# Attention with expert layers on one core: the sums of heads, their reciprocal and the division moved to other steps, and kept copies given fixed places

## The chip, the core and the metric

The kernel runs on one core of a Trainium2 chip. The core's engines run side by side, each in the order of its own queue: TensorE (matmuls; the profile's PE, its weight loads PEld), VectorE (DVE), ScalarE (ACT), GpSimd (POOL) and SyncE (SP), which issues DMAs. The metric is the device time of one execution in microseconds. Before the change the median of 14 runs is 1340.41 us (1339.85 to 1341.01).

## The reference

For `x` of 4 x 512 tokens by 512 features, in float32, the kernel computes `x + attention(xn) + experts(xn)`, where `xn` is the layer norm of `x`.

```
scores  = clip(einsum("bhqd,bhkd->bhqk", q, k), -80, 80), causal mask
weights = softmax(scores / sqrt(192))
out     = (weights @ v) of 16 heads, joined, @ W_O.T
output  = shared_expert(xn) + sum over the 3 best of 7 experts, weighted
expert  = (silu(x @ w1) * (x @ wg)) @ w2
```

Each head's `q` and `k` have 128 features from latent projections and 64 features with a rotary turn (the rope).

## The kernel before

The kernel has an expert part (to about 657 us) and an attention part (from there to the end). It is written in a language that allocates tiles and sets the semaphores. `keep(...)` pins an instruction behind everything that was written before it for its engine, so the order on TensorE, VectorE and ScalarE is that of the code. The GpSimd fetches `yg` (L1664) are kept too, yet the planner has placed them between other GpSimd instructions; where they stand is read from the trace.

**Products.** A 512-wide matrix product is done as seven half-size products (`seven`) in the order p = 0, 1, 5, 4, 6, 2, 3, each of 8 matmul passes, into three PSUM banks. Some of them have their bank copied to SBUF by ScalarE before the bank is added to (`kept`, L297 in the expert part; L1605 in the attention part). In the expert part every kept copy takes a buffer of the tag `v`, five in rotation. `unit_out` (L1045) adds the copies `v[3]` and `v[5]` in place and sends the sum to DRAM. If few units are needed, `y_few` is copied out by ScalarE (one half) and VectorE (the other half, L1386).

**Attention.** There are 32 steps, one for each pair of heads of each batch. Step i does, on TensorE: `scores(i)` (L1432 with 128 rows, then L1443 with 64 rows, into the banks `a0`, `a1`, `b0`, `b1`, `c` and one of a pool), the queries of step i+1 (`pqr` L1282, `pq` L1297), and `values` of step i-1 (`av` L1513). VectorE clips the six score tiles (L1461), ScalarE takes the exponentials (L1465), GpSimd masks (L1469) and adds up each head's weights along the keys (`su`, L1493 and L1497). VectorE also multiplies for the rope of step i+1 (L1268 and four of L1271), and GpSimd subtracts (L1272).

Four heads (two steps) make a project q = 0 to 15. `sums(q)` (L1532) has four matmuls with a column of 32 ones each, one for each head's `su`, into bank `a0`; VectorE takes the reciprocal (L1534); `spread_by_dma` (L1544) sends each head's 32 rows to 128 with four DMAs on SyncE's queue, 16 in all. `divide(q)` multiplies the four heads of `og` by it (L1566, four) and makes the factors of the seven products (L1572 and three of L1575). `project_out(q)` does the seven products (`op`, L230) into the banks `b1`, `c`, `b0`; ScalarE keeps four copies; VectorE adds three banks to `acc` (L1615), GpSimd adds the kept copies (L1612). `combine` (L1677, three on VectorE) adds expert rows that `fetch` (L1664, three indirect DMAs of GpSimd) brought. At the end of `project_out` SyncE loads the next project's factors `m` (L1585).

Order in the main loop, for an even step i = 2q+2: `scores`, `pqr`, `pq`, `weights`, then `sums(q)`, reciprocal and broadcasts, then the rope, `values`, `project_out(q-1)`. For the odd step 2q+3: `scores`, `pqr`, `pq`, `weights` with the rope behind the clips, `values`, and last `divide(q)`. Project 14 is divided in step 31; project 15 is summed inside `project_out(14)` (`last_heads`) and spread by matmuls.

Of the kernel before, what the change touches and what calls it, by code (L numbers as in the profile page):

```python
# [10 lines left out]
F32 = mybir.dt.float32  # L11
# [7 lines left out]
P = 128  # L19
B, S, D = 4, 512, 512  # L20
# [22 lines left out]
def kernel(  # L43
# [87 lines left out]
    def rows(src):  # L131
        return src.rearrange("(c p) f -> p c f", p=P)

    def ffn_in(at, name, w, x_of, between, step=FC):

        hp = fps.tile([P, S], F32, tag="h", name=f"h_{name}")
        gp = fps.tile([P, S], F32, tag="g", name=f"g_{name}")
        for ps, wt in ((hp, w[0]), (gp, w[1])):
            for f in range(FC):
                for c in range(DC):  # L140
                    keep(
                        nc.tensor.matmul(  # L142
                            ps[:, ts(f, P)],
                            wt[:, c, ts(f, P)],
                            x_of(c),
                            start=(c == 0),
                            stop=(c == DC - 1),
                        )
                    )
            if ps is hp:  # L150
                between()
        sl = sw.tile([P, S], F32, tag="v", name=f"sl_{name}", bufs=5)
        keep(nc.scalar.activation(sl, hp, AF.Silu))
        cols = [t.rearrange("p (c n) -> p c n", c=FC) for t in (gp, sl)]

        for f in range(0, FC, step):
            keep(nc.vector.tensor_mul(*(t[:, f : f + step] for t in (at, *cols))))
        return at
# [85 lines left out]
    def load_in(dst, src):  # L244

        with tc.issue_after(last[0]) if last[0] is not None else nullcontext():
            last[0] = nc.sync.dma_start(dst, src).ins
# [40 lines left out]
    def product(name, tag, a, w, done, hooks):  # L288

        banks = banks_of(tag, name)

        def kept(i, k):
            t = sw.tile([P, D], F32, tag="v", name=f"v{i}_{name}", bufs=5)
            keep(nc.scalar.copy(block(t), banks[k]))  # L297
            return block(t)

        copies = {0: (1, 0), 5: (2, 0), 4: (5, 2), 6: (3, 0)}  # L300
        sums = {1: 1, 2: 2, 3: 0}

        def then(p):
            if p in copies:
                done(copies[p][0], kept(*copies[p]))
            else:
                done(-p, banks[sums[p]])
            if p in hooks:
                hooks[p]()

        seven(a, w, banks, then, keep)
# [720 lines left out]
    def unit_out(s, a, w, hooks):  # L1032
        def to(t, n):
            at = (s * TPB + 2 * t) * P
            return y_d[at : at + 2 * P, half[n]].rearrange("(j p) f -> p j f", p=P)

        v = {}

        def done(i, src):
            v[i] = src  # L1040
            if i == -1:
                keep(V.tensor_add(v[1], src, v[1]))
                load_in(to(0, 0), v[1])
            elif i == 3:
                keep(V.tensor_add(v[3], v[3], v[5]))  # L1045
                load_in(to(1, 1), v[3])
            elif i == -2:
                keep(V.tensor_add(v[2], src, v[2]))
                load_in(to(0, 1), v[2])
            elif i == -3:  # L1050
                t = block(sw.tile([P, D], F32, tag="v", name=f"v4_r{s}", bufs=5))
                keep(nc.scalar.copy(t, src))
                load_in(to(1, 0), t)

        product(f"yr{s}", "y", a, w, done, hooks)
# [324 lines left out]
    with tc.If(used < SURE + 1) as few:  # L1380
        at = act_tile("few").rearrange("p c (t f) -> p t c f", t=TPB)[:, 0]
        at = ffn_in(at, "few", wbuf, lambda c: xT[SURE][:, c, :P], nothing, 1)
        y = sw.tile([P, D], F32, tag="v", name="y_few", bufs=5)
        yp = ffn_out("few", at, wbuf, keep)
        keep(nc.scalar.copy(y[:, half[0]], yp[:, half[0]]))
        keep(nc.vector.tensor_copy(y[:, half[1]], yp[:, half[1]]))  # L1386
        nc.sync.dma_start(y_d[ts(SURE * TPB, P), :], y)
    with few.Else():
        last[0] = None
# [63 lines left out]
    def weights(i, bank, then, behind):  # L1453

        pt = ap.tile([P, 5 * S], F32, tag="pt", name=f"pt_{i}")

        def clip(to, src):  # L1460
            keep(nc.vector.tensor_scalar(to, src, CLIP, -CLIP, ALU.min, ALU.max))  # L1461

        def exp(t):

            keep(nc.scalar.activation(t, t, AF.Exp, scale=QK_SCALE))  # L1465

        def mask(t, at, k=1, step=P):
            m = t[:, at : at + P]
            keep(nc.gpsimd.tensor_mul(m, m, tri))  # L1469

        for j in range(2):
            a = pt[:, ts(j, S)]
            clip(a, bank[j, 0])
            exp(a)
            mask(pt, PT[j, 0])
        half = 2 * P
        for j in (1, 0):
            clip(pt[:, PT[j, 2] : PT[j, 2] + half], bank[j, 2][:, :half])
        exp(pt[:, ts(2, S)])
        for j in range(2):  # L1480
            mask(pt, PT[j, 2])
        then()
        for j in range(2):
            t = pt[:, ts(3 + j, S)]
            clip(t, bank[j, 1])
            exp(t)
            mask(pt, PT[j, 1])
            mask(pt, PT[j, 3])
        behind()
        su = []  # L1490
        for j in range(2):
            t = ap.tile([P, S], F32, tag="su", name=f"su_{i}_{j}", bufs=4)
            keep(nc.gpsimd.tensor_copy(t[:, :P], pt[:, PT[j, 0] : PT[j, 0] + P]))  # L1493
            for kc in range(1, TPB):
                prev = pt[:, PT[j, 0] + P : PT[j, 0] + S] if kc == 1 else t[:, kc * P :]
                keep(
                    nc.gpsimd.tensor_add(  # L1497
                        t[:, kc * P :], prev, pt[:, PT[j, kc] : PT[j, kc] + PT_W[kc]]
                    )
                )  # L1500
            su.append(t)
        pts[i], sus[i] = pt, su
# [25 lines left out]
    def sums(q):  # L1528

        sb = bank("a0")(f"sb_{q}")  # L1530
        for j, su in enumerate(sus.pop(2 * q) + sus.pop(2 * q + 1)):
            keep(nc.tensor.matmul(sb[ts(j, 32), :], ones[:, :32], su, start=True, stop=True))  # L1532
        rc = ap.tile([P, S], F32, tag="rc", name=f"rc_{q}", bufs=1)
        keep(nc.vector.reciprocal(rc, sb))  # L1534
        return rc
# [21 lines left out]
    def divide(q):  # L1557

        o = og.pop(q)

        for cols in half if q == n // 2 - 1 else [slice(0, S)]:
            for j, rb in enumerate(spread[q]):
                keep(nc.vector.tensor_mul(o[:, j, cols], o[:, j, cols], rb[:, cols]))  # L1566
        a11, a21 = (o[:, 0:2, half[t]] for t in range(2))
        a12, a22 = (o[:, 2:4, half[t]] for t in range(2))
        x = [ap.tile([P, 2, S // 2], F32, tag=f"s{k}", name=f"s{k}_{q}") for k in (1, 2, 4)]

        def add(*t):
            keep(nc.vector.tensor_add(*t))  # L1572

        def sub(*t):
            keep(nc.vector.tensor_sub(*t))  # L1575

        firsts_of[q] = first_factors(add, sub, a11, a12, a21, a22, *x, a21)
# [104 lines left out]

    factors_of = {0: load_factors(0)}

    for i in range(n):
        more = i + 1 < n
        even = i % 2 == 0
        q = i // 2 - 1  # L1690
        held = scores(i)
        raw_copy, turn_q = rotary_query(i + 1, psum(f"pqr_{i + 1}")) if more else (nothing, nothing)
        qc_copy = query(i + 1, 0, psum(f"pq_{i + 1}_0")) if more else nothing
        weights(i, held, raw_copy, nothing if even else turn_q)
        qc_copy()
        if even and i > 0:
            spread_by_dma(q, sums(q))
        if even:
            turn_q()
        if i > 0:  # L1700
            values(i - 1, 0)
        if more:
            query(i + 1, 1, psum(f"pq_{i + 1}_1"))()
        if i < 2:
            project(2 + i, psum)
        if 1 < i < 5:
            turn_keys((2, 3, 1)[i - 2], psum)
        if i > 0:
            values(i - 1, 1)
        if even and i > 2:  # L1710
            project_out(q - 1, first_added=lambda: combine(q))
        if i == 1:
            combine(0)
        if even and i != 2 or i == 1:
            fetch((i + 1) // 2)
        if not even and i > 1:
            divide(q)

    q = n // 2 - 1

    def last_heads():
        combine(NTT - 1)
        values(n - 1, 0)
        values(n - 1, 1)
        last_rc.append(sums(q))

    last_rc = []
    project_out(q - 1, last_heads)
# [51 lines left out]
```

## Time and profile before

| what | value |
|---|---|
| median of 14 runs | 1340.41 us |
| the profiled execution's own time | 1340.64 us |
| its span (first to last instruction) | 1338.9 us |
| TensorE clock granted | 1.000 |
| an even step with `project_out` (989 to 1002 us of the trace, `scores` to `scores`) | 975.32 to 1002.83: 27.51 us |
| an odd step | 961.57 to 975.32: 13.75 us |
| VectorE busy in one pair of steps (949.64 to 990.90) | 33.29 of 41.26 us |
| GpSimd busy in the same pair | 35.05 us |
| ScalarE busy in the same pair | 13.46 us |
| TensorE busy, expert units (146.56 to 644.78) | 497.76 of 498.22 us |
| VectorE, one reciprocal 128x512 | 3.34 us |
| `rb` broadcasts: issue to landing, median | 2.0 us |
| kept copy 128x512 of ScalarE | 0.59 us |

A row of a timeline gives start, duration, engine, line, operation, output and inputs, and how many instructions were merged; a bracket gives the idle time before them and who ended it. The end of a matmul is modelled, so TensorE is best read from start to start: it is counted as busy also where one of four products that could run side by side runs alone. Of two engines that wait for each other, the later one is named. Idle time of VectorE or GpSimd costs nothing unless TensorE waits for them.

### The profile page before, as it was taken

The numbers are of one execution on the slowest core, as the hardware profiler recorded it, in microseconds if no ns is written. First come the engines' busy times: TensorE is split into PE (matmuls) and PEld (weight loads), VectorE is DVE, ScalarE is ACT, GpSimd is POOL, SyncE is SP. The second block draws the span as 40 slices with busy tenths as digits, with TensorE's granted clock in tenths as the row PEclk, the third lists the DMA queues.
The fourth block names the chain that finished last, engine by engine and source line by source line (L and its number), as shares of the span: only waits on it lengthen the run. The fifth ranks groups of instructions, "written<-read, shape, count | busy, mean of one in ns | idle before, by whom it ended". The sixth has DMA issues, their size and how long they took to land.

```text
span 1338.9 us, 17913 instructions
## 1 busy us (share of the span) xinstructions
PE 1329.2 (99%) x5949; PEld 991.9 (74%) x5949; DVE 974.7 (73%) x1426; ACT 406.2 (30%) x714; POOL 845.4 (63%) x952
## 2 busy tenths in 40 slices
PE   9999999999999999999999999999999999999998
PEld 8778888888888888877655666666666666666676
DVE  7679486666766677676468679877788777897775
ACT  3333222322223322212223423323333323233231
POOL 5113664554545465532277789888898888988883
PEclk9999999999999999999999999999999999999999
DMA  7850245766667675423401331243322333213332
GB/s 276 195 159 22 89 134 159 221 187 176 193 167 199 164 227 162 158 92 97 149 15 44 111 110 40 82 132 110 110 61 68 124 111 110 83 53 118 110 110 87
DMA packets 174100, 167.90 MB, mean 125 GB/s; under 512 B 57904, under 2 KB 136752, under 8 KB 174000
## 3 DMA queue, kind: packets, MB, share of 16 engines
q1 hardware_dynamic: 161264, 133.10, 33.7%
q0 software_dynamic: 12736, 33.57, 8.1%
q8 instruction: 49, 0.80, 0.3%
q14 instruction: 51, 0.42, 0.1%
HBM read 116.02 MB, written 34.87 MB: 113 GB/s over the span
## 4 chain that ended last, share of the span: by engine, by line
PE 94%; DVE 3%; issue 1%; DMA 1%; ACT 1%; SPq 0%; DVEq 0%; ACTq 0%
PE op L230 15%; PE yr L230 11%; PE hr L230 11%; PE av L1513 11%; PE gr L230 10%; PE sb L1432 4%; PE sa L1432 4%; PE pq L1297 4%; PE sa L1443 3%; PE pqr L1282 2%; PE sb L1443 2%; PE gs L230 2%; PE ys L230 2%; PE hs L230 2%; PE sb L1532 2%; PE h_s L142 1%
## 5 line engine op out<-in xcount | busy, mean ns | idle before, releaser
L182 POOL DMA_INDIRECT xs<-xn_d,idx_i x208 | 229.0, 1101 | 195.4 <-DVE xT L199 136.4
L1469 POOL TENSOR_TENSOR pt<-pt,tri 128x128 f32<-128x128 f32 x256 | 137.9, 559 | 68.0 <-ACT pt L1465 61.3
L1465 ACT ACTIVATE pt<-pt 128x512 f32<-128x512 f32 x160 | 94.4, 628 | 257.8 <-DVE pt L1461 256.8
L1513 PEld LDWEIGHTS av<-pt,xnT 128*128 128x128 f32 x512 | 95.4, 190 | 83.7 <-issue 47.7
L1513 PE MATMUL av<-pt,xnT 128*128 128x512 f32 (+3 forms) x512 | 149.8, 436 | 0.0
L1271 DVE TENSOR_TENSOR swap_q<-qraw,sinT 32x512 f32<-32x512 f32 x128 | 118.3, 924 | 1.7
L230 PE MATMUL op<-m,og 128*128 128x256 f32 x512 | 118.6, 379 | 0.5 <-DVE og L1566 0.5
L1497 POOL TENSOR_TENSOR su<-su,pt 128x256 f32<-128x256 f32 (+1 forms) x128 | 105.6, 825 | 10.0
L230 PEld LDWEIGHTS op<-m,og 128*128 128x128 f32 x512 | 96.0, 190 | 14.5 <-DVE og L1566 1.3
L1461 DVE TENSOR_SCALAR pt<-sa 128x512 f32<-128x512 f32 x64 | 41.1, 682 | 70.0 <-PE sa L1443 70.0
L1664 POOL DMA_INDIRECT yg<-y_d,pos_i x48 | 54.5, 1134 | 57.0 <-issue 50.7
L230 PE MATMUL op<-m,s 128*128 128x256 f32 x384 | 88.2, 379 | 0.1
L1497 POOL TENSOR_TENSOR su<-pt 128x384 f32<-128x384 f32 x64 | 83.8, 1310 | 0.0
L1612 POOL TENSOR_TENSOR acc<-acc,v 128x512 f32<-128x512 f32 x60 | 80.6, 1344 | 5.1 <-ACT v L1605 3.2
L230 PEld LDWEIGHTS op<-m,s 128*128 128x128 f32 x384 | 72.9, 190 | 10.3 <-issue 0.5
L1677 DVE SCALAR_TENSOR_TENSOR acc<-yg,wk,acc 128x512 f32<-128x512 f32 x48 | 56.7, 1181 | 19.1 <-POOL acc L1612 17.9
L1605 ACT COPY v<-op 128x512 f32<-128x512 f32 x64 | 37.5, 586 | 108.3 <-PE op L230 107.1
L1566 DVE TENSOR_TENSOR og<-og,rb 128x512 f32<-128x512 f32 (+1 forms) x68 | 68.6, 1069 | 0.6 <-PE rb L1552 0.2
L1615 DVE TENSOR_TENSOR acc<-op,acc 128x512 f32<-128x512 f32 x48 | 31.7, 686 | 49.5 <-POOL acc L1612 47.3
L230 PE MATMUL yr<-w,at_r 128*128 128x256 f32 x288 | 66.9, 380 | 0.3
L230 PE MATMUL gr<-xT,w 128*128 128x256 f32 x288 | 66.1, 379 | 0.0
L230 PE MATMUL hr<-xT,w 128*128 128x256 f32 x288 | 66.1, 379 | 0.0
(339 smaller groups left out, 2809.9 us busy)
## 6 DMA issues: line engine op xcount, KB each, us to landing
m<-m_d SPq DMA_DIRECT2D x112, 256.0 KB, 5.5
w<-in_L_ffn_W_dram SPq DMA_DIRECT2D x52, 512.0 KB, 4.2
rb<-rc SPq DMA_DIRECT2D x240, 64.0 KB, 2.0
w<-in_L_ffn_Wg_dram SPq DMA_DIRECT2D x26, 512.0 KB, 3.4
y_d<-v_yr SPq DMA_DIRECT2D x36, 256.0 KB, 2.4
y_d<-none SPq DMA_DIRECT2D x24, 256.0 KB, 4.7
acc<-in_L_attn_x_dram SPq DMA_DIRECT2D x16, 256.0 KB, 5.2
xn_d<-xp SPq DMA_DIRECT2D x16, 256.0 KB, 2.0
```

Source lines behind the costliest of these rows:

```text
L182: nc.gpsimd.indirect_dma_start(out=xs[blk][:, q, :], out_offset=None, in_=xn_d[:, :], in_offset=bass.IndirectOffsetOnAxis(ap=idx_i[:, q, b ...
L230: nc.tensor.matmul(banks[k][:, t, :], a[p][:, j, ts(t, P)], b[p][:, j, :], start=(k not in used), stop=(t == j == 1), skip_group_check=True,)
L1271: keep(nc.vector.tensor_mul(swap[there, :], raw[here, :], tables[1][here, :]))
L1432: nc.tensor.matmul(where(j, kc), lat(b, 1)[:, ts(kc, P)], qc[j][:, kc * P :], start=(kc != 3), stop=False,)
L1443: nc.tensor.matmul(where(j, kc), lat(b, 2)[r, ts(kc, P)], qr[r, kc * P :], start=False, stop=(kc != 1),)
L1465: keep(nc.scalar.activation(t, t, AF.Exp, scale=QK_SCALE))
L1469: keep(nc.gpsimd.tensor_mul(m, m, tri))
L1497: nc.gpsimd.tensor_add(t[:, kc * P :], prev, pt[:, PT[j, kc] : PT[j, kc] + PT_W[kc]])
L1513: nc.tensor.matmul(av[:, kc * P :], lat(b, 3)[:, ts(kc, P)], pt[:, PT[j, kc] : PT[j, kc] + PT_W[kc]], start=(kc == 0), stop=(kc == TPB - 1),)
L1566: keep(nc.vector.tensor_mul(o[:, j, cols], o[:, j, cols], rb[:, cols]))
L1612: keep(eng.tensor_add(block, block, v))
L1677: nc.vector.scalar_tensor_tensor(acc[:, g, :], yg, wk[:, g, k : k + 1], acc[:, g, :], ALU.mult, ALU.add)
```

## The change

The sums of project q move from the even step 2q+2 to the odd step 2q+3, directly behind `scores`; the reciprocal and the broadcasts go behind the clips of that odd step, in front of the rope. The division moves from the end of step 2q+3 to the even step 2q+4, behind the clips and in front of the rope; `project_out(q)` stays in step 2q+4. Project 14 is thus summed in step 31 and divided behind the loop. `su` has six buffers in place of four, and `s1`, `s2`, `s4` one in place of two. In the expert part each kept copy has a place of its own, one buffer each of `va` to `ve`, by the table `PLACE`; `unit_out` writes the sum of `v[3]` and `v[5]` into the factor tile `a[4]`; `y_few` is copied out whole by ScalarE.

```
+    def place(k, name):
+        return sw.tile([P, S], F32, tag=f"v{k}", name=name)
+    PLACE = {"h": {1: "b", 2: "c", 5: "b", 3: "a"}, "g": {1: "c", 2: "d", 5: "b", 3: "e"}}
+    PLACE["y"] = {1: "a", 2: "d", 5: "b", 3: "c", 4: "e"}
...
-        sl = sw.tile([P, S], F32, tag="v", name=f"sl_{name}", bufs=5)
+        sl = place("ab"[name in ("s1", "s3")], f"sl_{name}")
...
-            t = sw.tile([P, D], F32, tag="v", name=f"v{i}_{name}", bufs=5)
+            t = place(PLACE[tag][i], f"v{i}_{name}")
...
-                keep(V.tensor_add(v[3], v[3], v[5]))
-                load_in(to(1, 1), v[3])
+                keep(V.tensor_add(a[4], v[3], v[5]))
+                load_in(to(1, 1), a[4])
...
-        keep(nc.scalar.copy(y[:, half[0]], yp[:, half[0]]))
-        keep(nc.vector.tensor_copy(y[:, half[1]], yp[:, half[1]]))
+        keep(nc.scalar.copy(y, ffn_out("few", at, wbuf, keep)))
...
-            t = ap.tile([P, S], F32, tag="su", name=f"su_{i}_{j}", bufs=4)
+            t = ap.tile([P, S], F32, tag="su", name=f"su_{i}_{j}", bufs=6)
...
+        return sb
+
+    def inverse(q, sb):
         rc = ap.tile([P, S], F32, tag="rc", name=f"rc_{q}", bufs=1)
         keep(nc.vector.reciprocal(rc, sb))
         return rc
...
-        q = i // 2 - 1
+        q = (i - 3) // 2
         held = scores(i)
+        if not even and q >= 0:
+            sb = sums(q)
...
+        def behind_clips():
+            if q >= 0:
+                spread_by_dma(q, inverse(q, sb))
+            turn_q()
+
+        weights(i, held, raw_copy, nothing if even else behind_clips)
         qc_copy()
-        if even and i > 0:
-            spread_by_dma(q, sums(q))
+        if even and q >= 0:
+            divide(q)
         if even:
             turn_q()
...
-        if even and i > 2:
-            project_out(q - 1, first_added=lambda: combine(q))
+        if even and q >= 0:
+            project_out(q, first_added=lambda: combine(q + 1))
...
-        if not even and i > 1:
-            divide(q)
+    divide(q)
...
-        last_rc.append(sums(q))
+        last_rc.append(inverse(q, sums(q)))
```

More of the change, by code (lines that the diff above doesn't have):

```diff
@@ L1050, in done @@
             elif i == -3:
-                t = block(sw.tile([P, D], F32, tag="v", name=f"v4_r{s}", bufs=5))
+                t = block(place(PLACE["y"][4], f"v4_r{s}"))
                 keep(nc.scalar.copy(t, src))
@@ L1382 @@
         at = ffn_in(at, "few", wbuf, lambda c: xT[SURE][:, c, :P], nothing, 1)
-        y = sw.tile([P, D], F32, tag="v", name="y_few", bufs=5)
-        yp = ffn_out("few", at, wbuf, keep)
-        keep(nc.scalar.copy(y[:, half[0]], yp[:, half[0]]))
-        keep(nc.vector.tensor_copy(y[:, half[1]], yp[:, half[1]]))
+        y = place("b", "y_few")
+        keep(nc.scalar.copy(y, ffn_out("few", at, wbuf, keep)))
         nc.sync.dma_start(y_d[ts(SURE * TPB, P), :], y)
@@ L1568, in divide @@
         a12, a22 = (o[:, 2:4, half[t]] for t in range(2))
-        x = [ap.tile([P, 2, S // 2], F32, tag=f"s{k}", name=f"s{k}_{q}") for k in (1, 2, 4)]
+        x = []
+        for k in (1, 2, 4):
+            x.append(ap.tile([P, 2, S // 2], F32, tag=f"s{k}", name=f"s{k}_{q}", bufs=1))
         def add(*t):
@@ L1689 @@
         even = i % 2 == 0
-        q = i // 2 - 1
+        q = (i - 3) // 2
         held = scores(i)
+        if not even and q >= 0:
+            sb = sums(q)
         raw_copy, turn_q = rotary_query(i + 1, psum(f"pqr_{i + 1}")) if more else (nothing, nothing)
         qc_copy = query(i + 1, 0, psum(f"pq_{i + 1}_0")) if more else nothing
-        weights(i, held, raw_copy, nothing if even else turn_q)
+        def behind_clips():
[3 more added lines that the diff above has]
+        weights(i, held, raw_copy, nothing if even else behind_clips)
         qc_copy()
-        if even and i > 0:
-            spread_by_dma(q, sums(q))
+        if even and q >= 0:
+            divide(q)
         if even:
```

## The prediction

> **What bounds the kernel.** I read the page's busy line first, then the whole-run waits of the attention stage, then the timelines of TensorE, VectorE and GpSimd over one pair of head steps, and last the end of the run.
>
> ```profile
> PE 1329.2 (99%) x5949; PEld 991.9 (74%) x5949; DVE 974.7 (73%) x1426; ACT 406.2 (30%) x714; POOL 845.4 (63%) x952
> ```
>
> TensorE streams 1329.2 of 1338.9 us; the clock is 1.000 throughout. No TensorE work is removed, so a gain can only come from badly packed TensorE time, and a loss from a wait that makes TensorE stand. The change sits where the four sums of heads run. The timeline of TensorE in an even step:
>
> ```profile
> 982.09 1.12 PE L1282 MATMUL pqr<-xnT,qrT 128*128 128x512 f32 x2
> 983.05 1.02 PE L1297 MATMUL pq<-xnT,a_h 128*128 128x512 f32 x2
> 984.00 1.53 PE L1532 MATMUL sb<-su,ones 128*32 128x512 f32 x8
> 985.47 2.42 PE L1513 MATMUL av<-pt,xnT 128*128 128x512 f32 x8
> ```
>
> and its weight loads there (the bracket is idle time and its releaser):
>
> ```profile
> 984.00 0.15 PEld L1532 LDWEIGHTS sb<-su,ones 128*32 128x32 f32 x6 [0.76 <-DVE pt L1461]
> 984.49 0.14 PEld L1532 LDWEIGHTS sb<-su,ones 128*32 128x32 f32 x2 [0.33 <-POOL su L1497]
> ```
>
> Read start to start: `sums` holds TensorE 985.47 - 984.00 = 1.47 us. Three of its four 32-column products start together; the fourth waits for the last `su` of GpSimd and runs alone. TensorE counts as busy all the while. In step 2, where `su` is ready, the block is 707.71 - 706.71 = 1.00. The waits of the attention stage (us in total, times, longest) count the late steps, 13:
>
> ```profile
> PEld sb L1532 <- POOL su L1497: 4.4, 13, 0.4
> ```
>
> **The gain, step by step.** In the new place (odd step, behind `scores`) the operands are from the two steps before, so all four are ready: 1.47 - 1.00 = 0.47, 13 times = 6.1. The block also loses its two seams with full-array matmuls. `pq` lasts 984.00 - 983.05 = 0.95 in front of the sums and 970.15 - 969.29 = 0.86 in front of `av`: 0.09. The first `av` lasts 987.73 - 985.47 = 2.26 behind the sums and 972.31 - 970.15 = 2.16 behind `pq`: 0.10. In the new place the sums stand between `scores`' 64-row matmuls and `pqr`, a seam that is paid already (`pqr` first in line: 0.96 against 0.86). So 0.19, 15 times = 2.9. The seam from 64-row to 32-column form is in no row; its bounds are nothing and another 0.2 (+2.9 in all if paid, up to 1.4 less if it is free); I take one seam of 0.09, already in the `scores` tail. Sum: **-9.0**.
>
> The rule behind that row is in the Trainium skill, "TensorEngine Tiling (Array Packing)", Key Properties: changing the tiling mode drains the array, changing only the tile does not. By it the seam between the two small forms is paid and the gain is 9.0; if only the step to the full array drained, it would be 10.4. No run here shows that seam yet.
>
> The sums need bank `a0`, so they wait for the first clip of the same step. In the odd step VectorE stands idle (4.01 us) until `scores` is done with `a0` and clips at 967.13 to 967.8, before `scores` ends at 968.33: no wait. Behind that wait on TensorE stand `pqr`, `pq` and `av`, all with slack while it is zero.
>
> `y_few`: two half copies, 656.20 + 0.37 and 656.61 + 0.42, end at 657.03; one full copy of 0.59 (any 128x512 copy of ScalarE) ends at 656.79: **-0.2**. The places of the kept copies: in the expert stage TensorE is busy 497.8 of 498.2 us, so nothing can be won. Each place's old reader is at least one product (1.73 us) ahead of the new copy; cost nothing, and if a reader on VectorE came late, ScalarE's copy and then TensorE would wait. Same for `a[4]` (its product is p=4, the write comes behind p=6), `s` with one buffer and `su` with six.
>
> **The odd step after the change.** The reciprocal (3.34) goes in front of the rope. VectorE ends its clips at 970.28, would end the reciprocal at 973.6, the rope (now 970.26 to 974.70) at 978.0, and GpSimd's subtraction (1.3 to 1.7) at 979.7. `scores` of the next step wants `qr` at 979.73 and now 1.00 later, 980.7: 1.0 left, cost nothing. SP's sixteen broadcasts (10.01, last landing 2.0 after its issue) end near 985.7; the first division wants the first of them at 986.
>
> **The even step after the change.** Here VectorE carries clips, division, rope, and only then the bank adds, and GpSimd's queue holds behind the rope:
>
> ```profile
> 954.27 1.72 POOL L1272 TENSOR_TENSOR qr<-qr,swap_q 128x512 f32<-128x512 f32 x1
> 955.95 1.72 POOL L1612 TENSOR_TENSOR acc<-acc,v 128x512 f32<-128x512 f32 x1
> 957.83 1.35 POOL L1664 DMA_INDIRECT yg<-y_d,pos_i  x1 [0.16 <-issue]
> 959.48 1.01 POOL L1664 DMA_INDIRECT yg<-y_d,pos_i  x1 [0.30 <-issue]
> 960.52 1.28 POOL L1612 TENSOR_TENSOR acc<-acc,v 128x512 f32<-128x512 f32 x1
> ```
>
> The add at 960.52 must end before VectorE's add of bank `b0` (961.83, 0.69), and that before `scores` of the odd step writes `b0`, 2.57 after its start. Count from the start of the even step's `scores`: clips can begin at 5.56 (967.13 - 961.57); six clips 3.06 (983.24 to 986.30); the division; the rope 4.90 (948.29 to 953.19); hand-over 0.11, subtraction 1.27, add 1.72, two fetches 2.85 (957.67 to 960.52), add 1.28, bank add 0.69, hand-over 0.11: 8.03. The bank is wanted at 27.51 - 1.66 + 2.57 = 28.42. The division's price depends on GpSimd beside it: 8.51 in the odd step (974.73 to 983.24), at least 8 x 0.69 = 5.5 undisturbed. Nearest is the division beside mask work at the end of the run, then four sums beside `su` work:
>
> ```profile
> 1300.33 3.28 DVE L1566 TENSOR_TENSOR og<-og,rb 128x512 f32<-128x512 f32 x4
> ```
>
> 3.28 + 4.09 (979.23 to 983.32) = 7.4. Sum 5.56 + 3.06 + 7.4 + 4.90 + 8.03 = 28.95: TensorE stands 0.53 in each odd step. In 4 of 14 steps the fetches wait for the combine too (913.00 to 920.66 is 7.66 against 7.11): 1.07. Together 10 x 0.53 + 4 x 1.07 = **+9.6**; bounds 0 (division 5.5) and 14 x 1.7 = 24 (8.51). `project_out` itself keeps its time: the first product wants two divided heads at 15.4 - 1.6 = 13.8, they come at 10.3.
>
> The SBUF rule that speaks against the change is in the Trainium skill, "SBUF — State Buffer", two separate sides: VectorE operations with two SBUF inputs and GpSimd exclude each other, they do not share. The rows agree in kind (the same four multiplications take 3.28 or 4.47). An estimate by the rule, with VectorE losing all of every GpSimd instruction beside it, is the 8.51 and +24 in place of +9.6.
>
> **The end of the run.** Step 31 has no following head to cover its division:
>
> ```profile
> 1278.53 10.01 SPq L1544 DMA_DIRECT2D rb<-rc  x16
> ...
> 1288.64 5.26 SPq L1585 DMA_DIRECT2D m<-m_d  x7
> ```
>
> ```profile
> 1298.46 4.58 PE L1513 MATMUL av<-pt,xnT 128*128 128x512 f32 x16
> 1302.88 3.62 PE L230 MATMUL op<-m,og 128*128 128x256 f32 x16
> ```
>
> Before, `rb` for project 14 landed in step 30. Now its reciprocal runs in step 31. From the end T of `scores` 31 (1298.46): clips end at T+1.87 (1300.33), reciprocal T+5.21; one broadcast each 0.633 (10.01/16), landing 2.0 later: head 1 complete at T+11.7, multiplied at T+12.4; head 3 at T+16.7 and T+17.5. TensorE wants the first product at T+1.00+4.42 = T+5.4, so it stands 7.0, runs 1.73, wants the second at T+14.1 and stands 3.4 more. Nothing on TensorE can pass: its order is written out. **+10.4**.
>
> **The sum.** -9.0 - 0.2 + 9.6 + 10.4 = +10.8 on the profiled execution's 1340.64, which is 0.23 above the median of the runs: **1351.2**.
>
> **Rivals.**
> *No stall at `b0`.* The fetches are the only GpSimd instructions whose place the code doesn't fix. If the planner puts the second add ahead of one fetch (a fetch is 1.0 to 1.35), or the division runs nearer 5.5, the 9.6 is gone: +1.2, 1341.6, within 0.2%. For it: 0.53 is small. Against: in all steps of the trace both fetches stand ahead of that add. It decides from a division of 6.9 downwards.
> *Faster.* The one mechanism is a shorter wait at the end: with no stall at `b0` it decides below 6.5 us in place of 10.4. Broadcasts at 0.51 (the shortest of the 240 issues) land the last head 15 x 0.12 = 1.9 sooner, a free seam gives 1.4 and the expert stage's idle 0.46 at most: 1337.8, only the edge of it. Against it: the 16 issues at 10.01 are alike in every step.
> *All of the fetches ahead of the add,* or the division at 8.51: stalls of 1.7 and more, 1360 to 1366.
> *The change doesn't do what it says:* if the sums still run three and one, 6.1 of the gain is missing: 1357. Against: `su` of step 2q+1 ends about 25 us before.
>
> **How the numbers follow.** Forecast 0.57; no stall 0.28; faster 0.05; long stalls 0.06; sums unchanged 0.04. About 0.2% (2.7 us) is what a measurement here tells from no change. Faster 0.05, same 0.28, slower 0.67. The forecast alone reaches from 1345 to 1357; with the no-stall case and its seam the range is 1339.5 to 1357.
>
> **What the new profile would show.** `sums` of 1.0 us behind `scores`, in odd steps; even steps of 25.85 instead of 27.51; odd steps of 14.75 (no stall), 15.3 with it, with TensorE waiting for VectorE's bank add; and about 10 us of TensorE idle ahead of `op` behind step 31, released by the division. I would be wrong if the odd steps show no wait, if the end's idle time is under 7 us, or if the expert stage lengthens.

## The result, and the profile after

The changed kernel takes 1357.68 us (median of 6 runs, 1357.4 to 1359.63) against 1340.34 for the kernel before, measured beside it (28 runs): ratio 1.0132, 95% interval 1.0123 to 1.0142. It is slower, as forecast, but by 17.3 us and not by 10.8: the time lies 0.7 us above the top of the range.

The profiled execution took 1358.42 us with a span of 1356.6, 17.7 more than the span before. From the page of the changed kernel, busy time by engine:

```profile
PE 1327.5 (98%) x5949; PEld 992.0 (73%) x5949; DVE 938.7 (69%) x1425; ACT 408.2 (30%) x714; POOL 814.2 (60%) x952
```

TensorE is busy 1.7 us less than before in a span that is 17.7 longer, so the loss is standing time. The waits of TensorE in the changed kernel (us in total, times, longest):

```profile
PE sb L1439 <- DVE acc L1627: 12.5, 14, 1.3
PE op L238 <- issue: 4.3, 1, 4.3
PE op L238 <- DVE og L1576: 3.2, 3, 1.4
...
PE sa L1450 <- POOL qr L1281: 0.7, 1, 0.7
```

The first line is the stall at bank `b0`: 14 odd steps, each waiting for VectorE's bank add. The second and third are the end of the run. The last is new and was in no forecast. The two left out, at `warm` and `y_few`, were there before. The wait of the sums for GpSimd's `su` is gone.

A table by step, from the starts of `scores` in the two traces (us; "usual" is the value of most steps):

| | before | after | forecast |
|---|---|---|---|
| start of the first `scores` | 657.24 | 656.89 | -0.2 |
| even step, usual | 27.51 | 25.85 | 25.85 |
| odd step, usual | 13.76 | 15.78 | 15.3 |
| odd steps 13, 21, 29 | 13.76 | 16.34 to 16.37 | 15.8 |
| steps 2 and 3 together | 29.59 | 30.16 | |
| `scores` 31 to the end | 47.16 | 59.46 | +11.9 |

**An even step and what follows.** The timeline of VectorE in step 24, which starts at 1145.87 (start, duration, idle time and its releaser in the bracket):

```profile
1154.61 3.52 DVE L1576 TENSOR_TENSOR og<-og,rb 128x512 f32<-128x512 f32 x4
...
1162.19 0.94 DVE L1277 TENSOR_TENSOR qr<-qraw,cosT 128x512 f32<-128x512 f32 x1
1163.14 4.09 DVE L1280 TENSOR_TENSOR swap_q<-qraw,sinT 32x512 f32<-32x512 f32 x4
...
1174.47 1.29 DVE L1627 TENSOR_TENSOR acc<-op,acc 128x512 f32<-128x512 f32 x2 [2.81 <-POOL acc L1624]
```

and GpSimd's behind it:

```profile
1167.38 1.27 POOL L1281 TENSOR_TENSOR qr<-qr,swap_q 128x512 f32<-128x512 f32 x1 [0.69 <-DVE swap_q L1280]
1168.61 1.72 POOL L1624 TENSOR_TENSOR acc<-acc,v 128x512 f32<-128x512 f32 x1
1170.48 1.35 POOL L1676 DMA_INDIRECT yg<-y_d,pos_i  x1 [0.15 <-issue]
1172.13 1.01 POOL L1676 DMA_INDIRECT yg<-y_d,pos_i  x1 [0.30 <-issue]
1173.15 1.29 POOL L1624 TENSOR_TENSOR acc<-acc,v 128x512 f32<-128x512 f32 x1
```

GpSimd waits for the rope, makes one add, issues two fetches, makes the add that `b0` needs; VectorE stands 2.81 until then, and adds `b0` to `acc`. TensorE, in the odd step that starts at 1171.71:

```profile
1175.22 2.00 PE L1439 MATMUL sb<-qc,xnT 128*128 128x384 f32 x8 [0.76 <-DVE acc L1627]
...
1179.51 1.06 PE L1539 MATMUL sb<-su,ones 128*32 128x512 f32 x8
```

`sb` starts 3.51 behind the step's start, where an unhindered step has 2.58: 0.93 late. The block also lasts 2.00 where it lasts 1.90 unhindered. Together 1.03, which is 15.78 less 14.75. The sums hold TensorE 1.00, from 1179.51 to 1180.51, where `pqr` starts: all four products start together.

**The end.** TensorE behind `scores` 31, then VectorE:

```profile
1305.97 4.58 PE L1520 MATMUL av<-pt,xnT 128*128 128x512 f32 x16
1314.90 1.19 PE L238 MATMUL op<-m,og 128*128 128x256 f32 x2 [4.34 <-issue]
1317.48 3.75 PE L238 MATMUL op<-m,og 128*128 128x256 f32 x8 [1.39 <-DVE og L1576]
```

```profile
1306.85 3.35 DVE L1544 RECIPROCAL rc<-sb 128x512 f32<-128x512 f32 x1
1314.10 0.69 DVE L1576 TENSOR_TENSOR og<-og,rb 128x512 f32<-128x512 f32 x1 [3.91 <-DMA rb<-rc]
...
1321.82 0.69 DVE L1576 TENSOR_TENSOR og<-og,rb 128x512 f32<-128x512 f32 x1 [1.96 <-DMA rb<-rc]
```

Each multiplication waits for its broadcast, and the products wait for the multiplications. From `scores` 31 to the end it takes 12.30 more than before, of which 1.0 is the sums and 1.02 the stall of step 31 (`sb` 0.92 late and its block 0.10 longer): 10.3 is the price of the end.

### The profile page after: what moved, and what is told of

Same layout as the page of the kernel before. It is cut to its first block, busy times and chain, and to the rows that moved or that the text cites. A ratio compares the mean times of both kernels' runs of the same rounds, so it can differ in the third digit from the quotient of the medians.

```text
span 1356.6 us, 17928 instructions
## 1 busy us (share of the span) xinstructions
PE 1327.5 (98%) x5949; PEld 992.0 (73%) x5949; DVE 938.7 (69%) x1425; ACT 408.2 (30%) x714; POOL 814.2 (60%) x952
## 4 chain that ended last, share of the span: by engine, by line
PE 57%; DVE 19%; SPq 8%; issue 7%; POOL 5%; DMA 2%; ACT 1%; POOLq 0%; DVEq 0%; ACTq 0%
PE hr L238 11%; PE yr L238 10%; PE gr L238 10%; SPq L1554 8%; DVE pt L1468 4%; DVE og L1576 3%; DVE rc L1544 3%; DVE swap_q L1280 3%; PE gs L238 3%; PE sb L1439 3%; DMA rb<-rc 2%; PE ys L238 2%; PE hs L238 2%; POOL acc L1624 2%; PE op L238 2%
## 5 line engine op out<-in xcount | busy, mean ns | idle before, releaser
L238 PE MATMUL op<-m,og 128*128 128x256 f32 x512 | 121.5, 385 | 7.6 <-issue 4.3
L1280 DVE TENSOR_TENSOR swap_q<-qraw,sinT 32x512 f32<-32x512 f32 x128 | 107.8, 842 | 1.7
L1504 POOL TENSOR_TENSOR su<-su,pt 128x256 f32<-128x256 f32 (+1 forms) x128 | 95.0, 742 | 10.0
L1281 POOL TENSOR_TENSOR qr<-qr,swap_q 128x512 f32<-128x512 f32 x32 | 40.5, 1267 | 66.9 <-DVE swap_q L1280 66.9
L1504 POOL TENSOR_TENSOR su<-pt 128x384 f32<-128x384 f32 x64 | 76.8, 1200 | 0.0
L1439 PE MATMUL sb<-qc,xnT 128*128 128x384 f32 (+1 forms) x256 | 62.2, 386 | 12.5 <-DVE acc L1627 12.5
L1439 PEld LDWEIGHTS sb<-qc,xnT 128*128 128x128 f32 x256 | 42.0, 190 | 36.5 <-DVE acc L1627 22.3
```

The source lines that it names most:

```text
L238: nc.tensor.matmul(banks[k][:, t, :], a[p][:, j, ts(t, P)], b[p][:, j, :], start=(k not in used), stop=(t == j == 1), skip_group_check=True,)
L1280: keep(nc.vector.tensor_mul(swap[there, :], raw[here, :], tables[1][here, :]))
L1439: nc.tensor.matmul(where(j, kc), lat(b, 1)[:, ts(kc, P)], qc[j][:, kc * P :], start=(kc != 3), stop=False,)
L1504: nc.gpsimd.tensor_add(t[:, kc * P :], prev, pt[:, PT[j, kc] : PT[j, kc] + PT_W[kc]])
```

## The experiments

The first theory: TensorE stands in odd steps because VectorE's clips, division and rope, and then GpSimd's queue with two fetches in it, are one chain to bank `b0`; it stands at the end because sixteen broadcasts lie between the reciprocal and the division. The rivals stand with each experiment.

One thing has to be known to read the times. The twelve kernels ran on three chips on which the kernel before takes 1369 to 1394 us in place of 1340. There the expert stage, the part before the first `scores`, takes 20 to 47 us longer in every kernel and scatters from run to run by about as much as the effects sought. From the page of waits of the first experiment:

```profile
PE hr L238 <- issue: 26.9, 14, 4.9
```

These waits of the expert stage's products, for which the profile names no releaser ("issue"), are not in the profiles above. The attention stage doesn't scatter: from the first `scores` to the end the changed kernel takes 699.76 in the profile above and 699.75 in the experiments, and the kernel before 681.62. So each experiment is read by this **stage time** and its steps, and the ratio of its whole time to the kernel before on its chip stands beside it.

**1. The fetches behind the adds.**

```diff
-            keep(
+            with behind(nc.gpsimd):
                 nc.gpsimd.indirect_dma_start(
...
-            )
```

> The changed kernel, with the two or three fetches of a project placed behind GpSimd's four adds of that project, in place of between the first and the second. Theory (the fetches, 2.85 us of GpSimd's queue, make bank b0 late): the second add ends near 25.8 after the start of the even step's scores in place of 28.6, VectorE's add of b0 near 26.5, wanted at 28.4, so odd steps fall from 15.8 to 14.75 and from 16.35 to 14.75; all 14 stalls (about 16.5 us) go, step 3's 0.8 stays: 1341 us. Rival (the division and the rope alone are too long for the even step): the stalls shrink by half or less, 1350 us or more.

Stage time 684.16, 15.6 less than the changed kernel; ratio to the kernel before 0.9984, interval 0.9953 to 1.0015. GpSimd and TensorE in steps 24 and 25:

```profile
1202.99 1.27 POOL L1281 TENSOR_TENSOR qr<-qr,swap_q 128x512 f32<-128x512 f32 x1 [0.69 <-DVE swap_q L1280]
1204.22 3.39 POOL L1624 TENSOR_TENSOR acc<-acc,v 128x512 f32<-128x512 f32 x2
1208.31 2.62 POOL L1624 TENSOR_TENSOR acc<-acc,v 128x512 f32<-128x512 f32 x2 [0.70 <-DVE acc L1688]
```

```profile
1209.91 1.90 PE L1439 MATMUL sb<-qc,xnT 128*128 128x384 f32 x8
```

The first two adds now run back to back, the fetches from 1211.08, `sb` starts 2.58 behind the step's start without a wait, odd steps take 14.75, and the stall's line is gone from the waits. What is left is about 0.2 in each of the steps 13, 21 and 29, whose `b0` is still 0.1 late. VectorE's division and rope, unchanged here, are not too long by themselves; with the two fetches behind them the chain is.

**2. Matmuls for the broadcasts of step 31.** The kernel spreads project 15's reciprocals with four small matmuls already; this does so for project 14.

```diff
+    last_rc = []
...
-                spread_by_dma(q, inverse(q, sb))
+                rc = inverse(q, sb)
+                if more:
+                    spread_by_dma(q, rc)
+                else:
+                    last_rc.append(rc)
...
+    spread_by_matmul(q, last_rc.pop())
     divide(q)
...
-    last_rc = []
```

> The changed kernel, with project 14's reciprocals in step 31 spread over the partitions by four matmuls, as project 15's are, in place of sixteen DMAs. Theory (the sixteen broadcasts make the first product late, 10.25 us at the end): the matmuls cost TensorE about 1.7, and the products then wait only for the reciprocal and VectorE's division: 1349 us, 8 to 9 less than the changed kernel. Rival (VectorE's reciprocal and division hold the end, not the broadcasts): 1355 us or more.

From `scores` 31 to the end 51.52 against 59.46: 7.94 less; stage time 691.87; ratio 1.0027, 0.9999 to 1.0056. TensorE at the end:

```profile
1344.68 1.86 PE L1562 MATMUL rb<-rc,one_row 32*128 32x512 f32 x8
1346.58 3.89 PE L238 MATMUL op<-m,og 128*128 128x256 f32 x16
```

The matmuls start as soon as the reciprocal is done (VectorE ends it 1341.04 + 3.35 = 1344.39) and the product follows at once. So the end was the broadcasts, and 2.3 of the 10.3 are left, most of it the matmuls themselves (1.9).

**3. Both edits.**

> Both edits together: fetches behind the four adds, and project 14 spread by matmuls in step 31. If the two losses are apart and of the sizes that the trace shows (16.5 and 8.5): 1332.6 us, 7.7 less than the kernel before, which is the 9.3 of the sums and 0.3 of y_few less about 1.8 left at the end. If a loss only moves (the fetches' data then come late for the combine): 1337 us or more, with a wait of TensorE that the changed kernel doesn't show.

Stage time 676.47, 5.15 less than the kernel before; 0.9891, 0.9855 to 0.9927. Run again beside the changed kernel on another chip (the eleventh run):

> The two edits again (fetches behind the adds, matmuls in step 31), beside the changed kernel on the same chip. From the first scores to the end 676.5 us, 5.1 less than the kernel before, with y_few 5.4: ratio 0.996 if the places bring nothing in the expert stage, 0.991 to 0.994 if they bring 2.5 to 7 us.

Stage time 676.44; 0.9926, 0.9901 to 0.9951. The losses are apart and add: 699.76 - 15.60 - 7.94 = 676.22. No new wait of TensorE is in the trace. The 5.15 fall short of the 7.4 expected: 2.5 stay at the end where 1.8 were counted, and 0.8 in step 3 and 0.7 in the three special steps were not. This version is faster than both kernels. Its whole time gained more than the stage explains; experiments 4 and 10 come back to that.

**4. The places alone.** The kernel before with `place()`, `PLACE`, `a[4]` and the one copy of `y_few`, and nothing of the attention stage.

> The kernel before with only the kept copies' places, a[4], and y_few's one copy. Theory: the places cost and bring nothing, y_few 0.2 to 0.35 us: 1340.0 us, ratio 0.9998. Rival (the places alone shift the order of copies and cost part of the loss): 1342 us or more.

Stage time 681.44, as before (681.62): in the attention stage the places do nothing. But the whole time is 0.9939 of the kernel before, 0.9904 to 0.9973, 7 us less, which neither theory expected.

**5. The sums with ready operands, in the old place.**

```diff
-        for j, su in enumerate(sus.pop(2 * q) + sus.pop(2 * q + 1)):
+        heads = sus.pop(2 * q) + sus.pop(2 * q + 1)
+        for j, su in enumerate(heads[:2] + heads[:2]):
```

> The kernel before, with the four sums of a pair reading the two heads of its first step twice, so the second step's heads' sums are left out (their divisors are the first step's): all four operands are ready when the block begins. Theory (1.47 - 1.00 = 0.47 of the block is the fourth product running alone): even steps 27.04 in place of 27.51, odd steps 13.76 as before, 13 times, 6.1 us less: ratio 0.995. Rival (the four products of the old place are paced by something else, such as their weight loads or the drain): even steps stay at 27.5.

Even steps 27.04, odd 13.76; stage time 675.49, 6.13 less; 0.9953, 0.9924 to 0.9981. The trace around it:

```profile
1173.90 1.06 PE L1533 MATMUL sb<-su,ones 128*32 128x512 f32 x8
1174.90 2.42 PE L1513 MATMUL av<-pt,xnT 128*128 128x512 f32 x8
```

Start to start the block is 1.00 instead of 1.47, and both seams are still there: `pq` in front holds TensorE 0.95, and the first `av` 2.26. So 0.47 of the gain is the late fourth product, as read.

**6. The sums between two full-array products.** The kernel of experiment 3 with the sums behind `pqr` instead of in front of it.

```diff
-        if not even and q >= 0:
-            sb = sums(q)
         raw_copy, turn_q = rotary_query(i + 1, psum(f"pqr_{i + 1}")) if more else (nothing, nothing)
+        if not even and q >= 0:
+            sb = sums(q)
```

> The kernel with both edits (fetches behind the adds, matmuls in step 31), and the sums moved from in front of the rotary product to between it and the query product, so that they lie between two full-array matmuls again. Theory (two seams of 0.09 and 0.10 are paid there and spared in front): odd steps 14.94 in place of 14.75, 14 times, 2.7 us more than with both edits. Rival (the gain beyond the fourth product has another cause, or the seam is paid in either place): odd steps 14.75 to 14.80.

Odd steps 14.95; stage time 679.22, 2.75 more than experiment 3; 0.9947, 0.9919 to 0.9975.

```profile
1199.52 1.13 PE L1291 MATMUL pqr<-xnT,qrT 128*128 128x512 f32 x2
1200.57 1.06 PE L1539 MATMUL sb<-su,ones 128*32 128x512 f32 x8
1201.57 1.12 PE L1306 MATMUL pq<-xnT,a_h 128*128 128x512 f32 x2
```

`pqr` holds TensorE 1.05 (0.97 in experiment 3), and `pq` 0.96 (0.85). The two seams are worth 0.19 to 0.20, as forecast.

**7. A shorter division, fetches where the change has them.**

```diff
             for j, rb in enumerate(spread[q]):
+                if j == 0 and q < n // 2 - 2:
+                    continue
                 keep(nc.vector.tensor_mul(o[:, j, cols], o[:, j, cols], rb[:, cols]))
```

> The changed kernel, with one of the four multiplications of each division left out (the first head of each pair stays undivided, up to pair 13), 0.94 us of VectorE in each even step; the fetches stay where they were. Theory (VectorE's clips, division and rope, and then GpSimd's queue, are one chain to bank b0): the stall of each odd step shrinks by what was left out, from 1.05 to 0.1, so odd steps 14.8 to 14.9 and those of steps 13, 21 and 29 about 15.4: 13 to 14 us less than the changed kernel. Rival (GpSimd's own queue is the bound, whatever VectorE does): odd steps stay at 15.8.

Odd steps 15.04, steps 13, 21 and 29 15.61; stage time 691.18, 8.6 less than the changed kernel; 1.0062, 1.0033 to 1.009. VectorE in step 24, which starts at 1158.39, then GpSimd:

```profile
1167.14 2.65 DVE L1578 TENSOR_TENSOR og<-og,rb 128x512 f32<-128x512 f32 x3
...
1173.57 1.21 DVE L1277 TENSOR_TENSOR qr<-qraw,cosT 128x512 f32<-128x512 f32 x1
```

```profile
1177.27 1.92 POOL L1504 TENSOR_TENSOR su<-su,pt 128x256 f32<-128x256 f32 x2
1179.15 1.27 POOL L1281 TENSOR_TENSOR qr<-qr,swap_q 128x512 f32<-128x512 f32 x1
```

The rope starts 15.18 behind the step's start against 16.32 (1162.19 - 1145.87), and its longer first product (1.21 for 0.94) and others give some back: it ends at 20.5 instead of 21.4. GpSimd's subtraction comes only 0.75 sooner (20.76 against 21.51). GpSimd's own masks and `su` end 20.8 behind the step's start in both kernels: in the changed kernel GpSimd then stands 0.69 until the rope is done, here the rope is done 0.3 before them. The add of `b0` comes 0.74 sooner, and the stall shrinks from 1.03 to 0.29, by the same 0.74.

So the rival falls as the cause of the stall of 1.03: a shorter division takes most of it away. But it holds for the rest: with the shorter division GpSimd's own queue, with the fetches in it, is the bound, and the 0.29 left is GpSimd's. The expectation's 13 to 14 us was too much because it counted VectorE alone. The end also takes 60.53 here against 59.46, since the clock of TensorE stays halved for longer there (see the last section).

**8. The control: the kernel before with the fetches behind the adds.** The edit is that of experiment 1, in the kernel before.

> The kernel before with the fetches behind GpSimd's four adds, as a control. Theory (without the division in the even step bank b0 is ready long before it is wanted, so the place of the fetches is worth nothing): even steps 27.51, odd steps 13.76, ratio 1.000. Rival (fetches behind the adds win time by themselves): odd or even steps shorter by 0.1 or more, ratio 0.998 or less. In the expert stage this kernel is the one before, so its waits there stand against those of the kernels with places of their own, on the same chip if it is the same.

Stage time 681.62, all steps as before; 1.0027, 0.9995 to 1.006. Without the division in the even step the place of the fetches is worth nothing.

**9. Project 14 early.** The kernel of experiment 1 with project 14's sums and reciprocal in step 30.

```diff
-        if not even and q >= 0:
+        if not even and 0 <= q and more:
             sb = sums(q)
...
-            if q >= 0:
+            if q >= 0 and more:
                 spread_by_dma(q, inverse(q, sb))
...
             divide(q)
+        if i == n - 2:
+            sb = sums(q + 1)
         if even:
             turn_q()
+        if i == n - 2:
+            spread_by_dma(q + 1, inverse(q + 1, sb))
```

> The changed kernel with the fetches behind the adds, and project 14's sums and reciprocal in the even step 30, as the kernel before has them (behind the clips' step, the reciprocal behind the rope), spread by DMAs, so that its division has step 31 to run in. Theory (the end's 10.25 is the price of doing project 14's reciprocal in step 31): step 31 and the end take 47.2 us, as before, against 58.4 with the fetches' edit alone and 50.7 with the matmuls; step 30 grows from 25.85 to 27.5 by the late sums, and step 31 may stand up to 0.6 more at bank b0; from the first scores to the end 674.2 us, 2.2 less than with both edits, 7.4 less than the kernel before. Rival (VectorE's extra reciprocal in step 30 makes its bank add late): step 31 stands 2 us or more, 676 us or more.

Theory and rival both missed. Step 30 takes 27.04, and `sb` of step 31 starts only 0.5 late for `b0`, where the rival had 2; but `scores` 31 to the end takes 52.32 where theory had 47.2; stage time 679.28; 0.9963, 0.9934 to 0.9991. VectorE's row of the division:

```profile
1315.31 7.63 DVE L1576 TENSOR_TENSOR og<-og,rb 128x512 f32<-128x512 f32 x4
```

Behind the division and the rope the reciprocal comes late in step 30: it runs from 1300.4 to 1303.8, and the last broadcast is issued at 1313.2 and lands 4.3 later, at 1317.5. In the kernel before the reciprocal stands ahead of the rope and ends at 1278.5, 13.2 us ahead of the start of `scores` 31; here it ends 2.3 ahead of it. But the late broadcasts don't explain the row. One by one the multiplications take 4.94, 1.21, 0.94 and 0.77: the first, whose four broadcasts were issued by 1306.2, ends at 1320.25, 2.8 behind the landing of the last. TensorE stands 2.33 until it is done, and the clock is halved for 3.41 us behind that, which costs at most 1.7; the two are most of the 5.1 that theory missed. Beside the long multiplication GpSimd's masks take 0.44 to 0.46 each, where they take up to 0.90 beside the division of step 24, so GpSimd was not slowed there. Why VectorE was so slow in this one place is not shown. Matmuls (experiment 2) stay the better end.

**10. The changed kernel, and the places, once more.**

> The changed kernel itself, on a chip of the experiments. Theory: from the first scores to the end 699.8 us, 18.1 more than the kernel before, whatever the chip. If the places of the kept copies bring nothing where the expert stage waits for its weights, the ratio to the kernel before is 1.013; if they bring 2.5 to 7 us there, 1.008 to 1.011.

> The places, a[4] and y_few's one copy alone, again. If what the first run of them showed (7 us less than the kernel before, on a chip on which the expert stage waits for its weights) comes from the places: ratio 0.994 to 0.998 on such a chip, 1.000 on one that doesn't wait. If it was scatter of the expert stage: ratio 1.000 within its interval on any chip.

The changed kernel: stage time 699.75; 1.0115, 1.0075 to 1.0154. The places alone: stage time 681.52; 0.9975, 0.9944 to 1.0007. Taking from each kernel's difference of medians its difference of stage time leaves what lies in front of the attention stage. In the ten runs with the places that is -1.8 to -9.9 us: -5.0, -8.0, -9.9 and -7.0 on the first chip (experiments 1 to 4), -3.2 and -1.8 on the second (6, 7), -3.4, -2.2, -5.2 and -3.8 on the third (9, the changed kernel, 3 again, 4 again). In the two without them it is +0.8 and +2.9 (5, 8). So the places (with `y_few`'s copy, 0.2 to 0.35) seem to bring some us where the expert stage waits for its products, and nothing in the profiles of the result, where it doesn't wait. Each single interval is wide, and that of the second run of the places holds 1.000. By which wait they do it is not shown, nor that the expert stage waits for its weights, as the expectations put it; both stay open.

## Why the prediction was wrong in size and right in kind

**The gain of the sums: right.** Forecast 9.0. An even step loses 1.66 and an odd step gains 0.99, and experiment 3's steps give 8.7 net from `scores` 0 to `scores` 31; with the step-3 loss and the three special steps added back and the 1.0 of step 31 taken off, 9.1. Its two parts, 0.47 and 0.19, came out by themselves in experiments 5 and 6. The seam between the two small forms, which no row of the kernel before showed, is paid: the last 64-row block holds TensorE 0.97 in front of the sums (experiment 3), as long as in front of the full-array `pqr` (0.96, experiment 5). That agrees with the Trainium skill, "TensorEngine Tiling (Array Packing)", Key Properties, by which a change of the tiling mode drains the array; the 10.4 of a free seam did not come.

**`y_few` and the places: right** in the profiles of the result: the first `scores` starts 0.35 sooner.

**The end of the run: right.** 10.4 forecast, 10.3 measured, by the broadcasts (experiment 2).

**The stall at `b0`: right in place and mechanism, wrong in size. This is the step that failed.** Forecast 9.6, of 0.53 and 1.07 a step. Measured 10 x 1.04 and, in steps 5, 13, 21 and 29, 1.14 and three times 1.61: 16.3. The chain to `b0`, read in step 24 of the changed kernel (us from the step's start):

| term | forecast | measured |
|---|---|---|
| clips end | 8.62 | 8.72 |
| hand-over and division | 7.4 | 7.61 (0.03 + 7.58) |
| rope, to the end of VectorE's part | 4.90 | 5.07 |
| hand-over, subtraction, add, fetches, add, bank add, hand-over | 8.03 | 7.96 |
| `b0` free | 28.95 | 29.36 |
| `b0` wanted | 28.42 | 28.43 |

So 0.41 comes from three durations that were each 1 to 4% short, on a difference of 0.53; no single one is to blame. The rest, 0.10, was not in the sum: after a stand the first `sb` matmul costs 0.42 where it costs 0.32 in a row, so the block lasts 2.00 and not 1.90. Together 0.51 a step, in 13 of the 14 steps, is the 6.7 that were missing. What the sum had was a small difference of two numbers near 29, and an error of 1.4% in one of them doubled it. The prediction gave bounds of 0 to 24 for it, but the range's top, 1357.0, left it only 9.6 + 5.8 = 15.4. The lower bound was wrong too: it let a shorter division take the stall to nothing, and left out that GpSimd's own masks and `su` end 20.8 behind the step's start, ahead of the subtraction. With the fetches in their place that alone leaves 0.29 (experiment 7).

For the rule of the Trainium skill ("SBUF — State Buffer", two separate sides), by which VectorE and GpSimd exclude each other, the prediction put 8.51 for the division and 24 for the stalls. But 8.51 is a row of the odd step and was not worked out from the rule, so the measured 7.58 and 16.3 are no test of it. The multiplications do stretch beside GpSimd: 0.94 in step 24, 0.69 at 1319.17 at the end of the changed kernel, where the windows below show GpSimd not busy.

**Step 3: missed.** The prediction gave `qr` 1.0 us of slack in the odd steps and never looked at step 2, where the sums of project 0 had been. Without them it is 1.19 shorter (15.39 to 14.20), and GpSimd's masks and `su` of step 2 end at 18.10, behind them the rope's subtraction at 19.33, where `scores` 3 wants it about 18.6: 0.78, once, the last line of the waits.

**The rivals.** No stall at `b0`: the planner left the fetches where they were, so it did not come. Put behind the adds by hand (experiment 1) they nearly bring it: 1357.7 - 15.6 = 1342.1, where the prediction named 1341.6. The long stalls (1360 and more) did not come; that the sums are unchanged is refuted by their 1.00.

The terms as measured: -9.1 - 0.35 + 16.3 + 0.78 + 10.3 = 17.9; the spans differ by 17.7.

## What to carry to other kernels

Work that is moved to where its operands are ready gains what its own block lost, here 0.67 us a pair, but it moves its consumers too: count the queue of every engine behind the new place up to the first thing that TensorE wants back, and the work of other engines that joins that chain. When that count ends within a few per cent of the deadline, the small difference carries the error of the whole chain, and the range should be drawn from some per cent of the chain (its terms here were off by 1 to 4%), times the number of steps. Instructions of no urgency in an in-order queue are worth moving: here putting the fetches behind the adds gave back 15.6 us.

## What the runs showed of the hardware that was not expected

- A TensorE block that starts after a stand is 0.10 us longer: `sb` 2.00 against 1.90 unhindered, in all stalled steps.
- The granted clock drops after a stand of TensorE. Windows of the changed kernel's end (length, busy time and instructions of PE, PEld, DVE, ACT and POOL, PEclk, DMA share, GB/s):

```profile
1310.00:1315.00 5.00, 0.66 (x5) 0.47 (x3) 0.89 (x2) 0.58 (x1) 3.72 (x7) 0.92 0.31 79
1315.00:1320.00 5.00, 3.61 (x8) 2.30 (x9) 1.39 (x2) 0.00 (x0) 0.00 (x0) 0.50 0.42 105
```

  TensorE stands from 1310.55; 3.7 us later, at 1314.24, the clock is halved, for 6.83 us, and eight matmuls take 3.75 where they take 1.89. Here it costs little, since the next product waits for the division anyway; at the same place in experiment 7 it lasts 13.65 us, and the end is 1.07 longer. The rule behind the row is in the Trainium skill, "TensorE: Matmul & The Clock Gate", Part 1: the clock is halved after an idle window of about 3.4 us, and full again after as long a busy one. The case agrees in the length: in all traces the stretches of half clock within the program last 3.41 us, or two or four times that. It doesn't agree that TensorE must stand for so long: the half clock follows a stand of 2.33 in experiment 9 and one of 2.02 in the expert stage of experiment 5 (302.24 to 304.25).
- With one multiplication of VectorE left out in each even step, the next bound was only 0.75 away: GpSimd's own queue, which the wait of 0.69 in front of the subtraction had shown (experiment 7).
- The same expert stage took 657 us up to the first `scores` in the profiles of the result and 677 to 704 in those of the experiments, with waits of its `hr` products that the former don't show.
